# Moving the activation and the output step of an expert tile in the orders of two engines

## The chip, the cores and the metric

The kernel runs on one core of a Trainium2 chip. The metric is the device time of one execution in microseconds (us): the median of three runs before the change is 366.8 us (365.99 to 367.01). The engines that matter are TensorE (PE in the profile; PEld are its weight loads), VectorE (DVE), ScalarE (ACT), GpSimd (POOL), which starts the gathers and scatters, and SyncE (SP), which starts the other transfers. Each engine works through its own list of instructions in order, so an instruction that waits holds up all that stand behind it.

## What is computed

The input is x, 2048 tokens of 512 numbers. After a layer norm, two branches are added to x: an RWKV mixing layer (a recurrence over time for each channel) and a layer of eight experts, of which each token uses up to two, with four further "zero experts" that pass the token through.

```
xn = layernorm(x)
r, v, k = split(xn @ W_rvk.T)
y   = sigmoid(r) * wkv(time_decay, time_first, k, v)      # a recurrence over the 256 steps of each of 8 sequences
att = y @ W_out.T

probs = softmax(xn @ classifier_w.T)                      # 12 columns: 8 experts, 4 zero experts
idx   = top_k(probs + bias, 2);  w = probs[idx] * 1.5
g, u  = xn @ gate_w[e].T, xn @ up_w[e].T                  # 256 numbers for each expert e
out_e = (silu(g) * u) @ down_w[e].T
ffn   = sum over e of w[e] * out_e + xn * (sum of w over the zero experts)

return x + att + ffn
```

(In the code the reference's setup gives one sequence of 2048 tokens to the recurrence, which the kernel runs through in four blocks of 512.)

## The kernel before the change

**The start**, to about 61 us, normalises x, writes it to a scratch array xs, computes the routing, and sorts the token and expert pairs into tiles of 128 places, each tile belonging to one expert (two of them, "mixed", to two experts). The kernel works through TILES = 23 of them, and through a loop for more that is entered only if there are more.

**The long middle**, 61 to about 328 us, interleaves three streams of work.

- *Projections* (line 555, run from `pair`): k, v and r of the recurrence by a seven-product scheme. A step is one small matrix product into a PSUM bank (p1, p2, p3, pr) and a copy out of it on ScalarE (lines 574 to 599), with additions on VectorE (587, 600).
- *Scans* (`scan`, 16 units: four blocks by four groups of 128 channels): on VectorE a first part (lines 322 to 329), two exponentials on ScalarE (331, 332), then in one piece a run of VectorE work (338, 339, 340, 347 to 351) with an exponential of r on ScalarE (344) in the middle, then two reciprocals (354) and the product that gives yT (357). In the profile a scan's tiles are named obv, a, sums and yT.
- *Expert tiles*. For tile i: a gather of its rows on POOL (`gather`, 965); a copy xp on ScalarE (`flip`, 1032) and a transposing transfer on SP (1034); a copy xgT on ScalarE (`unite`, 1040); the gate and up products pg on TensorE (`up`, 1059, or 1011 for a mixed tile), 256 columns each, in one PSUM bank; the activation (`activate`): a tanh on ScalarE (1071) and two products on VectorE (1072, 1073) that read the bank and write act; the down products po (`finish`, 1007); a scaling copy yo on ScalarE (1091) and a scatter that adds it to the output (1095, POOL). Weights of the tile come by SP (986 for gate and up, 993 for down).

PSUM after the start: the bank of pg, from a pool "gu", exists once, so pg of tile i + 1 cannot begin before line 1073 of tile i has read it. The po tiles share a pool "ps_o" of two banks with the output rows pw.

**Output rows** (`attention`, line 1192 and 1180, tiles pw): y times W_out for 128 tokens, evicted on VectorE (1204) with the zero experts' share and added to the output by POOL (1165), or, for the last block, added to rows read back (1159, 1201, 1188) and written by SP.

**The order** of each engine in the middle is written out by hand (`manual_schedule`): the instructions of all engines stand in the order in which Python emits them. That order comes from a table: `plan(at, what, ...)` enters a piece of work with a planned time, and the table is sorted by it. `first_half(i)` (the fetch of weights, pg, the activation, a gather) is planned at 4 + spread * i, `second_half(i)` (unite of tile i + 1, flip of tile i + 2, finish of tile i - 1, the fetch of down weights) at 4 + spread * (i + 0.6). After the table a scheduler orders the rest, and may place some of it among the last pieces of the table.

Of the kernel before, what the change touches and what calls it, by code (L numbers as in the profile page):

```python
# [53 lines left out]
TILES = 23  # L54
# [9 lines left out]
def layer(ctx: ExitStack, tc: tile.TileContext, x, w_rvk, w_out, decay, first, cls, ebias, gu, down, out):  # L64
# [852 lines left out]
    to_i = const.tile([P, MAX_TILES], I32, tag="to_i", name="to_i")  # L917
    nc.vector.scalar_tensor_tensor(to_i, token, -float(P), empty, ALU.add, ALU.add)
    wplace = const.tile([P, MAX_TILES], F32, tag="wplace", name="wplace")
# [28 lines left out]
    st = {}  # L948
# [4 lines left out]
    def column(i):  # L953
        return seq[i] if i < TILES else 0

    def is_mixed(i):
        return i < TILES and seq[i] < MIXED
# [4 lines left out]
    def gather(i, token=token_i):  # L962

        xg = gathered.tile([P, C], F32, tag="xg", name=f"xg{i}")
        nc.gpsimd.indirect_dma_start(  # L965
            out=xg,
            out_offset=None,
            in_=xs,
            in_offset=bass.IndirectOffsetOnAxis(ap=token[:, column(i) : column(i) + 1], axis=0),
        )  # L970
        st.setdefault(i, {"w": [], "e": [], "d": []})["xg"] = xg

    def fetch(i, h=0, which=None):

        if which is None:
            k = column(i)
            which = owner_i[0:1, k, h : h + 1] if is_mixed(i) else which_i[0:1, k : k + 1]
        e = nc.values_load(
            which,
            engines=(SP,),  # L980
            min_val=0,
            max_val=E - 1,
            skip_runtime_bounds_check_because="a sum of E - 1 comparisons, or a number of one expert",
        )
        w = ewp.tile([P, CC, 2 * INTER], F32, tag="gw", name=f"gw{i}_{h}")
        nc.sync.dma_start(w, gu[bass.ds(e, 1)].rearrange("o p c n -> p (o c) n"))
        s = st.setdefault(i, {"w": [], "e": [], "d": []})
        s["w"].append(w)
        s["e"].append(e)

    def fetch_down(i, h=0):
        d = ewp.tile([P, IC, C], F32, tag="dw", name=f"dw{i}_{h}")
        nc.sync.dma_start(d, down[bass.ds(st[i]["e"][h], 1)].rearrange("o p c n -> p (o c) n"))
        st[i]["d"].append(d)
# [3 lines left out]
    def fetch_parts(what, i):  # L998

        while fetched[what] < min(ahead[i] + 3, len(parts)):  # L1000
            (fetch if what == "w" else fetch_down)(*parts[fetched[what]])
            fetched[what] += 1

    def product(i, out_, lhs, rhs, c, last):

        if not is_mixed(i):
            nc.tensor.matmul(out_, lhs[:, c, :], rhs[0][:, c, :], start=(c == 0), stop=(c == last))  # L1007
            return
        for g in range(P // GROUP):
            gs = slice(g * GROUP, (g + 1) * GROUP)  # L1010
            nc.tensor.matmul(  # L1011
                out_[gs],
                lhs[:, c, gs],
                rhs[g == P // GROUP - 1][:, c, :],
                start=(c == 0),
                stop=(c == last),
                tile_position=(0, g * GROUP),
            )

    def turn(i):  # L1020

        pt = bank("gu", f"px{i}", (CC, P))
        for c in range(CC):
            nc.tensor.transpose(pt[:, c, :], st[i]["xg"][:, c * P : (c + 1) * P], ident)
        xgT = wk1.tile([P, CC, P], F32, tag="xgT", name=f"xgT{i}")
        nc.scalar.copy(xgT, pt)
        st[i]["xgT"] = xgT
# [18 lines left out]
    def up(i, cs):  # L1046

        if 0 in cs:
            st[i]["pg"] = bank("gu", f"pg{i}", (2, INTER))
        pg = st[i]["pg"]  # L1050
        xgT, w = st[i]["xgT"], st[i]["w"]
        for c in cs:
            if is_mixed(i):
                product(i, pg, xgT, w, c, CC - 1)
                continue

            rs = slice(c * P, (c + 1) * P)
            for k in range(CC):
                nc.tensor.matmul(  # L1059
                    pg[:, c // IC, c % IC * P : (c % IC + 1) * P],  # L1060
                    w[0][:, k, rs],
                    xgT[:, k, :],
                    start=(k == 0),
                    stop=(k == CC - 1),
                )

    def activate(i):
        pg = st[i]["pg"]

        act = ex_p.tile([P, INTER], F32, tag="act", name=f"act{i}")  # L1070
        nc.scalar.activation(act, pg[:, 0, :], AF.Tanh, scale=0.5)  # L1071
        nc.vector.scalar_tensor_tensor(act, act, 1.0, pg[:, 0, :], ALU.add, ALU.mult)  # L1072
        nc.vector.tensor_mul(act, act, pg[:, 1, :])
        st[i]["act"] = act
        if not is_mixed(i):
            st[i]["actT"] = act.rearrange("p (c t) -> p c t", c=IC)

    def turn_act(i):
        pt = ps_o.tile([P, IC, P], F32, tag="o", name=f"pa{i}")
        for c in range(IC):  # L1080
            nc.tensor.transpose(pt[:, c, :], st[i]["act"][:, c * P : (c + 1) * P], ident)
        actT = wk1.tile([P, IC, P], F32, tag="actT", name=f"actT{i}")
        nc.scalar.copy(actT, pt)
        st[i]["actT"] = actT

    def finish(i, weight=wplace, to=to_i):
        po = ps_o.tile([P, C], F32, tag="o", name=f"po{i}")
        for c in range(IC):
            product(i, po, st[i]["actT"], st[i]["d"], c, IC - 1)
        yo = rows.tile([P, C], F32, tag="rb", name=f"yo{i}")  # L1090
        nc.scalar.activation(yo, po, AF.Identity, scale=weight[:, column(i) : column(i) + 1])
        k = column(i)

        def scatter(ps, index):
            nc.gpsimd.indirect_dma_start(  # L1095
                out=out,
                out_offset=bass.IndirectOffsetOnAxis(ap=index, axis=0),
                in_=yo[ps],
                in_offset=None,
                compute_op=ALU.add,  # L1100
            )


        if is_mixed(i):
            scatter(slice(0, P - GROUP), to[: P - GROUP, k : k + 1])
            held.append(lambda: scatter(slice(0, P), late_i[:, k : k + 1]))
        else:
            scatter(slice(0, P), to[:, k : k + 1])
        del st[i]
# [3 lines left out]
    def scatter_held():  # L1113
        while held:
            held.pop()()

    def first_half(i, n):

        fetch_parts("w", i)
        up(i, (0, 1))  # L1120
        if i > 0 and is_mixed(i - 1):
            turn_act(i - 1)
        up(i, (2, 3))
        activate(i)
        if i + 4 < n:
            gather(i + 4)
        scatter_held()

    def second_half(i, n):

        if i + 1 < n:
            unite(i + 1)
        if i + 2 < n:
            flip(i + 2)
        if i > 0:
            finish(i - 1)
        fetch_parts("d", i)
# [113 lines left out]
    def plan(at, what, *args):  # L1251
        table.append((at, iter([(what, *args)]) if args else what))
# [23 lines left out]
    spread = (total - 12) / TILES  # L1276
    for i in range(TILES):
        plan(4 + spread * i, first_half, i, TILES)
        plan(4 + spread * (i + 0.6), second_half, i, TILES)
    plan(6 + spread * (TILES - 1), read_xn, NTB - 2)  # L1280
    plan(7 + spread * TILES, read_xn, NTB - 1)
    plan(3 + spread * TILES, finish, TILES - 1)
    for _, work in sorted(table, key=lambda entry: entry[0]):
        todo = next(work, None)
        if todo:
            todo[0](*todo[1:])
# [10 lines left out]
    with tc.If(count > TILES):  # L1297
        with tc.For_i(TILES, MAX_TILES, 1) as i:
            cols = {}
            for name, a, dt in (  # L1300
                ("which", which_i, I32), ("token", token_i, I32), ("to", to_i, I32), ("weight", wplace, F32)
            ):
                cols[name] = small.tile([P, 1], dt, tag=f"col_{name}", name=f"col_{name}")
                nc.vector.tensor_copy(cols[name], a[:, bass.ds(i, 1)])
            gather(TILES, cols["token"])
            fetch(TILES, 0, cols["which"][0:1, 0:1])
            fetch_down(TILES)
            turn(TILES)
            up(TILES, range(CC))
            activate(TILES)  # L1310
            finish(TILES, cols["weight"], cols["to"])


    read_out(NTB - 1)
# [44 lines left out]
```

## Time and profile before

| | us |
|---|---|
| median of three runs | 366.8 (365.99 to 367.01) |
| the profiled execution | 366.11 |
| its span | 364.3 |
| TensorE busy | 354.8 (97%) |
| VectorE busy | 306.0 (84%) |
| ScalarE busy | 157.9 (43%) |
| tanh of a tile (1071), 23 times | 0.384 each |
| products of a tile (1072, 1073), 46 times | 0.415 and 0.420 each |
| scaling copy yo (1091), 23 times | 0.688 each |
| a scan's run on VectorE, 338 to 351, around 91.7 to 97.2 us | 5.5 |

How to read it: the span is the time from the first to the last recorded instruction of one execution; what lies around it is 1.8 us here. Busy time is the union of an engine's instructions. TensorE's matrix products are pipelined: an instruction in float32 is two passes, and the time that matters is the distance between the starts of passes (0.11 us for 128 columns, 0.22 for 256, 0.43 for 512), not the length of one. In a timeline a line holds the start, the length, the engine, the source line, the operation, and in brackets the idle time in front of it with what ended it; neighbouring instructions of one kind are one line ("x4"), and its length reaches to the end of the last.

### The profile page before, as it was taken

What the parts mean: (1) busy time and instruction counts of PE and PEld (TensorE: products, weight loads), DVE (VectorE), ACT (ScalarE), POOL (GpSimd) and SP (SyncE); (2) the same over time, 40 slices, a digit from 0 to 9 for tenths busy, and PEclk for the clock granted to TensorE, in tenths of its full rate; (3) what the DMA queues carried; (4) which work ended last, traced back from release to release, by engine and by line L of the source; (5) the groups of instructions that cost most, each with busy time, mean ns of one, the idle gap of its engine ahead of it and who ended that gap; (6) DMA issues with size and microseconds to landing.
All of it is one profiled execution on the core that took longest, in us unless ns stands there. A gap on an engine that the chain in (4) does not pass through costs nothing.

```text
span 364.3 us, 5277 instructions
## 1 busy us (share of the span) xinstructions
PE 354.8 (97%) x1840; PEld 253.9 (70%) x1840; DVE 306.0 (84%) x524; ACT 157.9 (43%) x303; POOL 89.5 (25%) x118
## 2 busy tenths in 40 slices
PE   8999999999989999999999999999999999999996
PEld 3565468798856877558866788887777888864444
DVE  5889989988999597898699959799968599879971
ACT  1667122345455345553535454546543446432000
POOL 6000200421302332332321242333223332122130
PEclk9999999999999999999999999999999999999999
DMA  8999941895848999799999599878989978934782
GB/s 270 395 376 352 347 146 21 321 288 126 222 151 258 271 291 269 182 281 259 314 285 235 164 259 254 247 134 289 245 285 252 266 160 187 349 56 57 172 129 106
DMA packets 47133, 84.46 MB, mean 232 GB/s; under 512 B 26497, under 2 KB 26881, under 8 KB 43329
## 3 DMA queue, kind: packets, MB, share of 16 engines
q1 hardware_dynamic: 39792, 64.05, 54.7%
q0 software_dynamic: 7312, 20.06, 25.6%
q8 instruction: 15, 0.25, 0.3%
q14 instruction: 14, 0.11, 0.1%
HBM read 63.25 MB, written 19.27 MB: 227 GB/s over the span
## 4 chain that ended last, share of the span: by engine, by line
PE 51%; DVE 25%; ACT 3%; DMA 2%; issue 2%; POOL 1%; SPq 0%; DVEq 0%; ACTq 0%
PE pg L1059 16%; PE p L555 12%; PE pw L1192 8%; PE po L1007 6%; DVE sums L354 5%; PE pr L555 5%; DMA gw<-in_gu_dram 2%; DVE sums L340 2%; DVE sums L338 2%; DVE obv L326 2%; DVE sums L349 1%; DVE yT L357 1%; DVE sums L350 1%; DVE a L351 1%; PE po L1011 1%
## 5 line engine op out<-in xcount | busy, mean ns | idle before, releaser
L1059 PEld LDWEIGHTS pg<-xgT,gw 128*128 128x128 f32 x672 | 78.2, 192 | 4.1 <-issue 1.9
L1059 PE MATMUL pg<-xgT,gw 128*128 128x128 f32 x672 | 79.0, 275 | 0.4 <-DMA gw<-in_gu_dram 0.4
L1095 POOL DMA_INDIRECT out_dram<-yo,to_i x23 | 39.4, 1713 | 145.2 <-DMA out_dram<-yo,to_i 31.0
L1192 PE MATMUL pw<-wout_sb,yT 128*128 128x512 f32 x120 | 54.5, 595 | 0.8 <-DVE xrows L1204 0.4
L354 DVE RECIPROCAL sums<-sums 128x256 f32<-128x256 f32 x32 | 54.7, 1731 | 0.0
L1192 PEld LDWEIGHTS pw<-wout_sb,yT 128*128 128x128 f32 x120 | 22.2, 190 | 26.9 <-issue 25.4
L1007 PE MATMUL po<-dw,act 128*128 128x512 f32 x84 | 39.5, 592 | 0.0
L965 POOL DMA_INDIRECT xg<-xs,token_i x23 | 26.2, 1138 | 45.8 <-DVE empty L916 25.2
L1071 ACT ACTIVATE act<-pg 128x256 f32<-128x256 f32 x23 | 8.8, 384 | 65.7 <-PE pg L1059 60.5
L1072 DVE SCALAR_TENSOR_TENSOR act<-act,pg 128x256 f32<-128x256 f32 x23 | 9.5, 415 | 26.3 <-ACT act L1071 26.3
L338 DVE TENSOR_TENSOR_SCAN sums<-obv,state,a 128x512 f32<-128x512 f32 x16 | 20.5, 1281 | 7.1 <-ACT obv L332 7.0
L1040 ACT COPY xgT<-xq 128x1024 uint16<-128x1024 uint16 x22 | 25.6, 1162 | 0.0
L555 PE MATMUL p<-S,T 128*128 128x256 f32 x96 | 24.9, 382 | 0.3 <-ACT v L578 0.3
L1007 PEld LDWEIGHTS po<-dw,act 128*128 128x128 f32 x84 | 16.0, 190 | 13.3 <-issue 12.2
L555 PE MATMUL p<-S,wrvk 128*128 128x256 f32 x96 | 24.7, 380 | 0.4 <-DVE S L408 0.4
L555 PE MATMUL p<-xnT,wrvk 128*128 128x256 f32 x96 | 24.7, 379 | 0.0
L1032 ACT COPY xp<-xg 128x1024 uint16<-128x1024 uint16 x22 | 23.0, 1047 | 1.0 <-DMA xg<-xs,token_i 1.0
L555 PEld LDWEIGHTS p<-S,T 128*128 128x128 f32 x96 | 17.9, 190 | 6.8 <-issue 2.4
L340 DVE TENSOR_TENSOR_SCAN sums<-obv,state,a 128x512 f32<-128x512 f32 x16 | 20.5, 1284 | 0.6
L555 PEld LDWEIGHTS p<-S,wrvk 128*128 128x128 f32 x96 | 17.7, 190 | 4.2 <-issue 1.2
L326 DVE TENSOR_TENSOR_SCAN obv<-wdec,state,k 128x512 f32<-128x512 f32 x16 | 20.5, 1279 | 0.0
L555 PEld LDWEIGHTS p<-xnT,wrvk 128*128 128x128 f32 x96 | 17.8, 190 | 3.4 <-issue 1.2
(262 smaller groups left out, 571.8 us busy)
## 6 DMA issues: line engine op xcount, KB each, us to landing
gw<-in_gu_dram SPq DMA_DIRECT2D x25, 1024.0 KB, 7.9
dw<-in_down_dram SPq DMA_DIRECT2D x25, 512.0 KB, 4.3
x<-in_x_dram SPq DMA_DIRECT2D x16, 256.0 KB, 5.3
xs<-x SPq DMA_DIRECT2D x16, 256.0 KB, 4.2
wrvk<-in_w_rvk_dram SPq DMA_DIRECT2D x3, 1024.0 KB, 8.5
xrow<-xs SPq DMA_DIRECT2D x8, 256.0 KB, 5.9
out_dram<-xrow POOLq DMA_DIRECT2D x8, 256.0 KB, 8.1
xrows<-xs SPq DMA_DIRECT2D x8, 256.0 KB, 6.2
```

What stands on the lines that cost most here:

```text
L326: nc.vector.tensor_tensor_scan(o2, w.to_broadcast([P, TB]), k, s[:, 0:1], ALU.add, ALU.max)
L338: nc.vector.tensor_tensor_scan(sq, bs, a2, s[:, 3:4], ALU.add, ALU.mult)
L340: nc.vector.tensor_tensor_scan(sp, bvs, a2, s[:, 4:5], ALU.add, ALU.mult)
L354: nc.vector.reciprocal(den[:, hs], den[:, hs])
L555: nc.tensor.matmul(dst, rows_(k), a[:, k, :], start=(first and k == 0), stop=(k == 1), skip_group_check=True,)
L965: nc.gpsimd.indirect_dma_start(out=xg, out_offset=None, in_=xs, in_offset=bass.IndirectOffsetOnAxis(ap=token[:, column(i) : column(i) + 1] ...
L1007: nc.tensor.matmul(out_, lhs[:, c, :], rhs[0][:, c, :], start=(c == 0), stop=(c == last))
L1032: nc.scalar.copy(xp, st[i]["xg"].bitcast(U16).rearrange("p (c h) -> p h c", h=2))
L1040: nc.scalar.copy(xgT.bitcast(U16).rearrange("p c (t h) -> p c t h", h=2), st[i]["xq"].rearrange("p (h c) t -> p c t h", h=2),)
L1059: nc.tensor.matmul(pg[:, c // IC, c % IC * P : (c % IC + 1) * P], w[0][:, k, rs], xgT[:, k, :], start=(k == 0), stop=(k == CC - 1),)
L1095: nc.gpsimd.indirect_dma_start(out=out, out_offset=bass.IndirectOffsetOnAxis(ap=index, axis=0), in_=yo[ps], in_offset=None, compute_op=ALU ...
L1192: nc.tensor.matmul(po, yT[b][:, c, j * P : (j + 1) * P], wout_sb[:, c, :], start=(c == 0), stop=(c == CC - 1),)
```

## The change

The activation leaves `first_half` and gets an entry of its own in the table, 3.6 planned us after the start of the half, and the scaling copy and the scatter leave `finish` as a new function `send`, planned 1.9 after the half that holds the down products. TensorE's work keeps its order but for the end.

```diff
-    def finish(i, weight=wplace, to=to_i):
+    def finish(i):
         po = ps_o.tile([P, C], F32, tag="o", name=f"po{i}")
         for c in range(IC):
             product(i, po, st[i]["actT"], st[i]["d"], c, IC - 1)
+        st[i]["po"] = po
+
+    def send(i, weight=wplace, to=to_i):
+        po = st[i]["po"]
         yo = rows.tile([P, C], F32, tag="rb", name=f"yo{i}")
         nc.scalar.activation(yo, po, AF.Identity, scale=weight[:, column(i) : column(i) + 1])
...
         up(i, (2, 3))
-        activate(i)
         if i + 4 < n:
             gather(i + 4)
...
     for i in range(TILES):
         plan(4 + spread * i, first_half, i, TILES)
+
+        plan(4 + spread * i + 3.6, activate, i)
         plan(4 + spread * (i + 0.6), second_half, i, TILES)
+        if i > 0:
+            plan(4 + spread * (i + 0.6) + 1.9, send, i - 1)
...
     plan(3 + spread * TILES, finish, TILES - 1)
+    plan(5 + spread * TILES, send, TILES - 1)
...
-            finish(TILES, cols["weight"], cols["to"])
+            finish(TILES)
+            send(TILES, cols["weight"], cols["to"])
```

What it does to the orders, read from the two built programs:

- VectorE: the two products of a tile stand behind up to ten instructions that stood behind them (9 at tile 1, 6 at tiles 6, 9, 10 and 19, 10 at tile 14, 7 at tile 22, none at tiles 7, 11, 17 and 20). At tiles 1, 9, 14, 19 and 22, for example, these include a scan's run from 338 to 351.
- ScalarE: the tanh stands behind up to five instructions more, yo behind up to three.
- POOL: one scatter, that of tile 6, stands behind the additions of two output rows (1165) that stood behind it. The rest is as before.
- SP: as before.
- TensorE: as before, but that the first two products of the very last row half (pw_last, line 1180) stand in front of po of the last tile instead of at the end, and two products of pw of row tile 11 stand behind the branch to the loop of further tiles instead of in front of it.

## The prediction

> **What bounds the kernel now.** I read the busy shares first, then the sums by stretch, the waits, and the timeline around the few places where TensorE stood still. The profiled execution took 366.11 us, 364.3 of it the span; the runs' median is 366.8.
>
> ```profile
> PE 354.8 (97%) x1840; PEld 253.9 (70%) x1840; DVE 306.0 (84%) x524; ACT 157.9 (43%) x303; POOL 89.5 (25%) x118
> ```
>
> ```profile
> 186.00:252.00 66.00, 65.67 (x363) 53.33 (x362) 57.87 (x83) 31.56 (x61) 19.88 (x15) 1.00 0.87 232
> 252.00:322.00 70.00, 70.00 (x393) 57.13 (x394) 57.82 (x81) 33.89 (x64) 18.63 (x14) 1.00 0.88 238
> ```
>
> The second view gives, after the length of a stretch, the busy time of PE, of its weight loads, DVE, ACT and POOL. From 186 to 322 us PE is full: 135.67 of 136.00. A later VectorE or ScalarE costs nothing until PE waits for it, and an earlier one can give back only what PE now waits.
>
> ```profile
> ACT act L1071 <- PE pg L1059: 60.5, 20, 5.4
> ...
> DVE act L1072 <- ACT act L1071: 26.3, 13, 3.8
> ```
>
> These are the waits that the change goes for: ScalarE stands 60.5 us in front of the tanh, VectorE 26.3 us in front of the first product after it. Neither is PE's time.
>
> **What it takes away.** What PE loses I read from the starts of its groups: four passes of line 555 follow each other 0.86 us after their start, four of line 1192 after 1.72 (both in the chain of waits). After 75 us there are six places of note. (a) At 90.84 us line 555 starts 0.50 late, for the copy of v (L578), and the moved tanh holds 0.27 of ScalarE in front of that copy (90.16 to 90.43): 0.25 falls away. (b) pg of tile 3 starts at 107.97, and 105.72 + 0.86 is 106.58: 1.39, for xgT (L1040), which stands behind the two exponentials of a scan and so behind its L328 and the products of tile 2 (102.35). With that pair (two of 0.42 us, 0.8) out of the way, and the run in front of it earlier by 0.5 (1.4 gained at its start, 0.9 taken back for tile 1's pair, below), xgT ends 1.3 earlier, at 106.6, while PE now comes 0.6 later (below), at 107.2: all of 1.39 goes. (c) pg of tile 4, 119.96 against 118.55 + 0.86: 0.55, for weights whose transfer follows xp (L1032) and its transpose through SP's queue; those move with xgT, 1.3 earlier, PE only 0.8: it goes. (d) pw at 195.86 against 194.57 + 0.86: 0.43, for xrow (L1204), behind tile 10's products (191.62). (e) pg of tile 16, 251.97 against 250.88 + 0.86: 0.23, like (b). (f) pw at 346.84 against 344.51 + 1.72: 0.61, for the row evictions L1204 behind the last scan; there PE now comes later than VectorE. Together 0.25 + 1.39 + 0.55 + 0.43 + 0.23 + 0.61 = 3.46 us. That is the whole purse.
>
> **What it adds.** No instruction is new; 23 tanhs of 0.38 us, 46 products of 0.42 and 23 copies yo of 0.69 move. Two things wait for the products: the next tile's pg, since the pool "gu" holds one bank and L1073 is its last reader, and the tile's own po (L1007). In the order of VectorE the pair now often stands behind a scan's whole run, L338 to L351, which was queued behind it.
>
> ```profile
> 90.84 1.13 PE L555 MATMUL p<-S,T 128*128 128x256 f32 x4 [0.33 <-ACT v L578]
> ...
> 91.69 1.27 DVE L338 TENSOR_TENSOR_SCAN sums<-obv,state,a 128x512 f32<-128x512 f32 x1
> ...
> 96.12 3.73 PE L1059 MATMUL pg<-xgT,gw 128*128 128x128 f32 x32
> ...
> 96.50 0.74 DVE L351 SCALAR_TENSOR_TENSOR a<-obv,cfac,sums 128x512 f32<-128x512 f32 x1
> ```
>
> (g) Tile 2. The run can start when L332 ends (89.63 + 0.63 = 90.26), 1.4 earlier than 91.69; so L351 ends at 97.24 - 1.4 = 95.84, and with the pair (0.88 from the first's start to the second's end, 90.56 to 91.44) the bank is free at 96.7. PE comes at 96.12 - 0.25 = 95.87. New wait: 0.9. It makes PE 0.6 late at tile 3, which (b) and (c) turn into 1.3 early.
>
> ```profile
> 181.46 1.28 DVE L338 TENSOR_TENSOR_SCAN sums<-obv,state,a 128x512 f32<-128x512 f32 x1 [1.03 <-ACT obv L332]
> ...
> 186.36 0.75 DVE L351 SCALAR_TENSOR_TENSOR a<-obv,cfac,sums 128x512 f32<-128x512 f32 x1
> ...
> 186.69 3.73 PE L1059 MATMUL pg<-xgT,gw 128*128 128x128 f32 x32
> ```
>
> (h) Tile 10. Here the run cannot start earlier against PE: its exponentials stand behind a ScalarE copy (L599, 180.01) that waits for PE. L351 ends 0.42 after PE comes for pg (187.11 against 186.69); with the pair (0.8 behind it) that is 1.2. What (b) and (c) gave is gone. (i) Tile 15 is a tie: VectorE's run ends 1.1 after PE comes (L351, 242.37 against 241.28) but starts some 2 earlier (it loses a 2.35 us wait for the tanh at 234.13), and two short operations follow: 0 to 0.5, I take 0.1.
>
> ```profile
> 322.08 0.37 ACT L595 COPY r<-pr 128x256 f32<-128x256 f32 x1 [0.48 <-PE pr L555]
> ...
> 323.54 1.28 DVE L338 TENSOR_TENSOR_SCAN sums<-obv,state,a 128x512 f32<-128x512 f32 x1 [0.70 <-ACT obv L332]
> ...
> 326.17 1.88 PE L1007 MATMUL po<-dw,act 128*128 128x512 f32 x4
> ...
> 328.09 0.75 DVE L351 SCALAR_TENSOR_TENSOR a<-obv,cfac,sums 128x512 f32<-128x512 f32 x1
> ```
>
> (j) The last tile is the largest. Its products ran at 321.63 to 322.51, while VectorE waited for the exponentials anyway; in the new order they follow L351. That run is tied to PE by the copy at 322.08. L351 ends at 328.84, the pair at 329.65; po of tile 22, at 326.17 until now, has the first two steps of the very last row tile put in front of it (four passes of 256 columns, 0.86) and so is reached at 327.03. New wait: 2.6. The two steps are work taken from the end, neither gain nor loss. What follows, 19 steps of line 1192 of 0.86 each, has no other slack than (f).
>
> New waits: 0.9 + 1.2 + 0.1 + 2.6 = 4.8. The sum: 4.8 - 3.46 = 1.3 us, 364.3 to 365.6 for the span, 366.8 to 368.1 for the median.
>
> **Costed at nothing.** The later yo and its scatter: the bank of po is one of two and is wanted again a tile (11 us) later, and scatters wait on POOL anyway (yo of 174.23 is scattered at 187.99, after 8.56 us for an earlier transfer). Tile 6's scatter now stands behind two row additions (L1165), before it in front. POOL's next gather moves with this: ScalarE waited once, 0.96 us at 239.57, for a gather. Without the cover I bound this part by that wait from above, and by its loss from below: -1 to +1.
>
> [...] The starts decide: line 1059 starts a pass every 0.11 us (32 in 3.57) though a load takes 0.19, so loads overlap and their share is no measure of room. [...]
>
> **The rivals.** One, on the other side: the run on VectorE comes earlier than I allow, and (g), (h), (i) don't arise. For it: 26.3 us of waits leave VectorE. Against: at tile 10 and at the end the run is released by ScalarE copies that wait for PE, not for VectorE. 366.8 - 3.46 + 2.6 = 365.9, and 363.3 if the end's wait too were covered; it decides if L351 of that run ends 1.2 us earlier against PE. Two, a draw: one wait of the size of (h) fails to come, 366.9. Three, worse: VectorE's lateness spreads. Reckoned as above, the pair is within about 1 us of PE at tiles 6, 7 and 11; one half to one microsecond at two of them adds 1.5: 369.6. That the change doesn't do what it says is no rival of weight: in the orders of the built program 21 of 23 tanhs, 19 pairs and 17 copies yo stand behind work that was behind them, up to ten instructions for a pair.
>
> **The numbers.** Forecast 368.1, chance 0.42 (own range 367.6 to 368.8); the draw 0.30; worse 0.14; faster side 0.14. One measurement tells about 0.3%, 1.1 us: slower starts at 367.9, faster ends at 365.7. Slower: 0.36 of the forecast's and all of the worse, 0.50; faster: 0.12 of the faster side; same: 0.38. The range, with the -1 to +1 of POOL's part: 366.0 to 369.7.
>
> **What would show it.** Each in the profile after: ScalarE's 60.5 and VectorE's 26.3 us in front of the moved lines mostly gone, with no gain in span; PE waiting for DVE act (L1073) at pg near 96 and 186 us and at po near 327, the last by 2.6; no wait near 107, 119 and 347. I am wrong if PE's last wait is under 1.5 us, if waits at pg come at more than four tiles, or if a gather or weight transfer becomes what PE waits for.

## The result, and the profile after

The changed kernel takes 369.77 us, the median of 19 executions (367.71 to 372.87); the kernel before took 365.99 in 19 executions beside it (364.88 to 368.49). The ratio is 1.0105, with a 95% interval of 1.0082 to 1.0127: slower by 1%, or 3.8 us. The forecast was 368.1 with a range up to 369.7, so the direction was right, the size was not, and the result lies just beyond the range. The forecast counted from 366.8; from there the range reached 2.9 us up, and 3.8 was measured against the kernel beside it, so the miss of the change is larger than that of the time.

The profiled execution took 372.09 us, 370.3 of it the span, 6.0 us more than the 364.3 before. First the page: busy time of each engine, and in 40 equal slices of the span the clock that TensorE was granted, in tenths.

```profile
PE 358.1 (97%) x1840; PEld 255.7 (69%) x1840; DVE 306.4 (83%) x524; ACT 156.8 (42%) x303; POOL 87.3 (24%) x118
...
PEclk9899999999999999999999999999999999998999
```

The number of passes is the same (1840), yet PE's busy time has grown from 354.8 to 358.1. Work that doesn't change and takes longer points at the clock, and the last line has two slices with an 8, the second of all and the fourth from the end; the profile before has none.

Next the waits (in total, times, longest), for what the change aimed at.

```profile
ACT k L595 <- PE p L555: 25.2, 10, 8.4
...
DVE sums L338 <- ACT obv L332: 17.9, 8, 6.7
...
DVE act L1072 <- ACT act L1071: 16.1, 6, 4.6
...
ACT act L1071 <- PE pg L1059: 4.1, 3, 2.8
```

ScalarE's 60.5 us in front of the tanh are down to 4.1, VectorE's 26.3 in front of the first product to 16.1. The waits went elsewhere: ScalarE now stands 25.2 us in front of its copy of k (8.1 before), and VectorE 17.9 in front of a scan (7.0 before). Neither sets the end. PE does, and in its timeline (start, length, engine, line, operation, in brackets the idle time in front and what ended it) the new waits stand where they were looked for:

```profile
98.87 1.35 PE L1059 MATMUL pg<-xgT,gw 128*128 128x128 f32 x10 [0.89 <-DVE act L1073]
...
108.55 1.03 PE L555 MATMUL p<-xnT,wrvk 128*128 128x256 f32 x4
109.50 3.64 PE L1011 MATMUL pg<-gw,xgT 128*32 128x512 f32 x32
...
189.06 3.81 PE L1059 MATMUL pg<-xgT,gw 128*128 128x128 f32 x32 [1.30 <-DVE act L1073]
...
243.69 2.58 PE L1059 MATMUL pg<-xgT,gw 128*128 128x128 f32 x21 [0.33 <-ACT yo L1095]
...
328.33 1.03 PE L1183 MATMUL pw_last<-wout_sb,yT 128*128 128x256 f32 x4
331.88 3.48 PE L1007 MATMUL po<-dw,act 128*128 128x512 f32 x4 [2.52 <-issue]
335.16 14.97 PE L1195 MATMUL pw<-wout_sb,yT 128*128 128x512 f32 x34
```

By the starts of the passes these are 1.06, 1.47, 0.50 and 2.68 us late: 5.71. At 109.50 pg of tile 3 no longer waits for xgT: 0.95 after the start of the four passes in front of it, against 2.25 before (105.72 to 107.97). The line of before:

```profile
107.97 1.50 PE L1011 MATMUL pg<-gw,xgT 128*32 128x512 f32 x12 [1.22 <-ACT xgT L1040]
```

The bracket at 331.88 names "issue", that at 243.69 a copy; VectorE's own timeline shows the true releaser of both. At the last tile the pair stands behind L351, at the end of the scan's run, and its second product ends at 331.78, 0.10 before po starts. At 243.69 it ends 0.26 before pg starts, as it does at 98.87 and 189.06.

```profile
243.01 0.42 DVE L1073 TENSOR_TENSOR act<-act,pg 128x256 f32<-128x256 f32 x1
...
327.60 1.28 DVE L340 TENSOR_TENSOR_SCAN sums<-obv,state,a 128x512 f32<-128x512 f32 x1
...
330.25 0.75 DVE L351 SCALAR_TENSOR_TENSOR a<-obv,cfac,sums 128x512 f32<-128x512 f32 x1
330.91 0.41 DVE L1072 SCALAR_TENSOR_TENSOR act<-act,pg 128x256 f32<-128x256 f32 x1
331.36 0.42 DVE L1073 TENSOR_TENSOR act<-act,pg 128x256 f32<-128x256 f32 x1
```

Now the length at 331.88: four passes of po take 3.48 us, and the same four took 1.88 before. The sums by stretch tell why. They are cut where the record of the clock changes, at steps of 3.41 us; the columns are the stretch, its length, busy time (and instructions) of PE, its weight loads, DVE, ACT and POOL, the granted clock, the DMA share and GB/s.

```profile
325.34:328.75 3.41, 3.41 (x10) 1.70 (x9) 3.02 (x3) 1.80 (x4) 2.06 (x1) 1.00 0.00 0
328.75:332.16 3.41, 0.89 (x4) 0.49 (x3) 3.26 (x7) 0.00 (x0) 0.00 (x0) 1.00 0.59 77
332.16:335.57 3.41, 3.41 (x5) 1.35 (x4) 3.38 (x3) 0.17 (x1) 1.54 (x1) 0.50 0.37 40
335.57:338.98 3.41, 3.41 (x9) 1.50 (x8) 3.37 (x6) 1.60 (x3) 0.93 (x1) 1.00 0.21 37
```

PE stands 2.52 us in the second stretch, and for the whole third stretch its clock is one half: five passes, where the busy stretches, the first and the fourth, hold ten and nine. The starts of those passes are 0.85 us apart instead of 0.43; together the starts lose 1.77 us. The wait is paid once as idle time and again as a slow restart.

The other 8 belongs to 11.31 to 14.72 us, the same 3.41 us at half clock, in the first transposes. The change doesn't touch them; by 70 us PE is 1.83 us behind the kernel before. So 5.8 of the 6.0 us between these two profiles are accounted for: 1.83 at the start, 5.71 of new waits, 1.77 of slow passes behind the last one, less the 3.5 that were taken away.

Each execution lists its span and mean clock. One stretch of 3.41 us at one half in 366 is a mean of 0.995, two make 0.991, so the executions can be sorted by the number of falls. Median span, and executions in brackets:

| kernel | clock 0.997 and over | 0.993 to 0.996 | 0.991 and under |
|---|---|---|---|
| before (beside the experiments) | 364.0 (39) | 366.4 (13) | none |
| after | 366.4 (7) | 368.4 (9) | 370.3 (3) |

At full clock the change costs 2.4 us; the remaining 1.4 of the 3.8 is that 12 of its 19 executions have one or two falls, and only 13 of 52 of the kernel before.

### The profile page after: what moved, and what is told of

Its sections match the earlier page's. It is cut to its first block, busy times and chain, and to the rows that moved or that the text cites. A ratio compares the mean times of both kernels' runs of the same rounds, so it can differ in the third digit from the quotient of the medians.

```text
span 370.3 us, 5289 instructions
## 1 busy us (share of the span) xinstructions
PE 358.1 (97%) x1840; PEld 255.7 (69%) x1840; DVE 306.4 (83%) x524; ACT 156.8 (42%) x303; POOL 87.3 (24%) x118
## 5 line engine op out<-in xcount | busy, mean ns | idle before, releaser
L1007 PE MATMUL po<-dw,act 128*128 128x512 f32 x84 | 41.1, 613 | 2.5 <-issue 2.5
L338 DVE TENSOR_TENSOR_SCAN sums<-obv,state,a 128x512 f32<-128x512 f32 x16 | 20.6, 1285 | 18.1 <-ACT obv L332 17.9
L965 POOL DMA_INDIRECT xg<-xs,token_i x23 | 24.4, 1060 | 46.9 <-DVE empty L916 25.2
L1072 DVE SCALAR_TENSOR_TENSOR act<-act,pg 128x256 f32<-128x256 f32 x23 | 9.5, 414 | 16.3 <-ACT act L1071 16.1
L555 PEld LDWEIGHTS p<-S,T 128*128 128x128 f32 x96 | 17.9, 190 | 6.4 <-issue 2.2
L1095 ACT ACTIVATE yo<-po,wplace 128x512 f32<-128x512 f32 x23 | 15.9, 692 | 10.2 <-PE po L1007 10.2
```

The costliest lines, as they stand in the source:

```text
L338: nc.vector.tensor_tensor_scan(sq, bs, a2, s[:, 3:4], ALU.add, ALU.mult)
L555: nc.tensor.matmul(dst, rows_(k), a[:, k, :], start=(first and k == 0), stop=(k == 1), skip_group_check=True,)
L965: nc.gpsimd.indirect_dma_start(out=xg, out_offset=None, in_=xs, in_offset=bass.IndirectOffsetOnAxis(ap=token[:, column(i) : column(i) + 1] ...
```

## The experiments

Eight kernels, in two groups of four, each group on one chip beside the kernel before. The theory, called W: what is lost lies at the last tile, in PE's wait for products that stand behind a scan's run on VectorE, and in the clock that falls behind this wait. Rivals: the clock falls by chance whatever PE does (C); the loss is spread over the tiles (S).

**The last tile alone in its old place.**

```diff
         up(i, (2, 3))
+        if i == TILES - 1:
+            activate(i)
...
-        plan(4 + spread * i + 3.6, activate, i)
+        if not (i == TILES - 1):
+            plan(4 + spread * i + 3.6, activate, i)
```

> The changed kernel, but the last tile's tanh and products stand where they stood before, directly after its pg; all else as changed. Theory W (wait and clock): what the changed kernel lost by its end is the wait of po of tile 22 (2.68 us by the starts of PE's passes) and, in the executions whose granted clock falls to half behind that wait, another 1.77 us (the four passes that start 0.85 instead of 0.43 apart). Both go; the wait of 0.61 us at line 1192, which the later PE had covered, comes back. From the changed kernel's executions at clock 1.0 (span about 366.2): 366.2 - 2.68 + 0.61 = 364.1, time about 365.9, ratio to the kernel before 0.998 to 1.001, and no fall of the clock in the last 40 us. Rival C (the clock falls by chance, whatever PE does): the fall behind 330 us stays in half or more of the executions, time 366.5 to 367.5. Rival S (the loss is spread over the tiles): the time stays within 1 us of the changed kernel, 368.8 or more.

Measured: 366.43 us (12 executions), ratio 1.0018 (0.9999 to 1.0037); 11 of 12 at full clock, the profiled span 364.4. PE reaches po of tile 22 without a wait; the two steps of the very last row tile that the change puts in front of it stand at the end again, which by itself is neither gain nor loss.

```profile
326.28 1.88 PE L1007 MATMUL po<-dw,act 128*128 128x512 f32 x4
```

The loss is gone, so it was the last tile's. The time is half a microsecond above what W gave; the other 22 tiles together are no gain: the waits at pg of tiles 2, 10 and 15 (1.06, 1.46 and 0.30 by the starts, 2.8 together) eat the 2.8 taken away elsewhere, and the row wait of 0.52 near 346 us is back as expected. S falls.

**The last tile alone late, the rest as before.**

```diff
         up(i, (2, 3))
-        activate(i)
+        if i < TILES - 1:
+            activate(i)
...
+        if i == TILES - 1:
+            plan(4 + spread * i + 3.6, activate, i)
```

> The kernel before, but the last tile alone has its tanh and products later; yo, the scatters and all other tiles as before. Theory W: po of tile 22 waits 2.6 to 3.4 us for the products, 0.61 of it comes back at line 1192; where the clock falls behind the wait, 1.8 more. Span 364.3 + 2.0 to 2.8 = 366.3 to 367.1 at full clock, 368.1 to 368.9 with the fall, time 368 to 370.5, ratio 1.006 to 1.012. Rival C: 1.005 to 1.008 and no more falls of the clock than the kernel before shows beside it. Rival S: no difference of note, below 1.003.

Measured: 368.73 us (6 executions), ratio 1.0080 (1.0058 to 1.0102), within W's bounds, and at the upper end of C's: one late tile of 23 gives 2.8 us. The profile has the same wait and no fall behind it.

```profile
330.14 1.96 PE L1007 MATMUL po<-dw,act 128*128 128x512 f32 x4 [2.52 <-issue]
```

Here the steps of the clock's record cut the wait in two:

```profile
326.20:329.61 3.41, 1.42 (x6) 0.72 (x4) 3.27 (x5) 0.00 (x0) 2.29 (x1) 1.00 0.20 18
329.61:333.03 3.42, 2.89 (x7) 1.44 (x8) 3.41 (x3) 0.69 (x1) 0.00 (x0) 1.00 0.37 59
```

PE works 1.42 us in the first of the two stretches, against 0.89 where the clock fell. So the wait costs its 2.68 us in both, and the clock falls behind it in one of the two profiles alone. They differ in where the idle time lies against the steps: from 329.36 to 331.88 us within one step there, from 327.62 to 330.14 across the edge at 329.61 here. Two of six executions show a clock of 0.994, which by itself doesn't tell W from C.

**The wait filled with work.**

```diff
         po = ps_o.tile([P, C], F32, tag="o", name=f"po{i}")
+        if i == TILES - 1:
+            for c in (0, 1, 2):
+                nc.tensor.matmul(po, st[i]["xgT"][:, c, :], st[i]["d"][0][:, 0, :], start=True, stop=True)
```

> The changed kernel with three matmuls of 128x512 added in front of po of tile 22 (six passes of 0.43 us, 2.58 us), from xgT and the first part of dw into the same bank, which the first real pass overwrites; the result is the same. PE's wait of 2.5 us is filled with work, so that the products are as late as before but PE never stands. Theory W: the clock does not fall behind 330 us, and every execution costs what the changed kernel's did at full clock: span 366.0 to 366.7, time about 368.0, ratio 1.004 to 1.007. Rival C (the fall has nothing to do with the wait): as the changed kernel, a median near 369.8, ratio 1.009 to 1.012, with falls as often. If the added passes are themselves in the way (they start later than reckoned), the time is above 369.8 at full clock.

Measured: 369.53 us (6 executions), ratio 1.0097 (1.0073 to 1.0121). The time is W's miss and lies in C's range, but not for C's reason: the added passes took the place of four passes of 256 columns of the very last row tile, which went back to the end (0.86 us), and still left a wait of 0.76, so at full clock it is 367.6 instead of 366.4. But the clock did what W says: in the profile it doesn't fall behind 330 us (its one fall lies in the second of the 40 slices, between 9.2 and 18.5 us, at the start), and five of six executions are at 0.999 or 1.0, where 7 of 19 of the changed kernel were. The lines are the granted clock in 40 slices, the added passes and po:

```profile
PEclk9899999999999999999999999999999999999999
...
328.13 2.74 PE L1090 MATMUL po<-dw,xgT 128*128 128x512 f32 x6
331.63 1.99 PE L1007 MATMUL po<-dw,act 128*128 128x512 f32 x4 [0.76 <-DVE act L1073]
```

Filling a wait with useless work kept the clock and won nothing here.

**A longer wait.**

```diff
         nc.vector.tensor_mul(act, act, pg[:, 1, :])
+        if i == TILES - 1:
+            for _ in range(4):
+                nc.vector.tensor_copy(act, act)
```

> The changed kernel with four more VectorE copies of act of tile 22 onto itself behind its products (0.42 us each by the rows of the products, 1.7 in all); the result is the same. PE's wait in front of po of tile 22 grows from 2.7 to 4.4 us. Theory W (a long enough wait lets the clock fall): the granted clock falls behind the wait in nearly every execution, where it fell in somewhat over half of the changed kernel's; span 366.2 + 1.7 + 1.8 = 369.7, time 371.3 to 372.0, mean clock 0.995 or below in five of six. Rival C (the clock falls by chance): 0.995 in a fifth of the executions, as in the kernel before beside it, span 367.9, time 369.4 to 370.2.

Measured: 372.14 us (6 executions), ratio 1.0130 (1.0084 to 1.0176). Five of six executions are at 0.995 or below, three of them at 0.991. C, which had 369.4 to 370.2 and a fifth of the executions, falls. The copies took 0.3 us each, so the wait grew by 1.3:

```profile
331.45 3.75 PE L1007 MATMUL po<-dw,act 128*128 128x512 f32 x4 [3.83 <-issue]
```

and in the sums by stretch:

```profile
326.57:329.98 3.41, 1.05 (x5) 0.57 (x3) 3.27 (x6) 0.00 (x0) 1.92 (x1) 1.00 0.31 32
329.98:333.39 3.41, 1.94 (x3) 0.94 (x4) 3.27 (x7) 0.00 (x0) 0.00 (x0) 0.50 0.26 45
333.39:336.80 3.41, 3.41 (x6) 1.34 (x5) 3.34 (x5) 0.69 (x1) 0.60 (x1) 0.50 0.00 0
```

The half clock lasts two steps here: the wait reaches into a second one, in which PE is busy for only 1.94 us at the slow rate, and the step behind it is at one half as well.

**The tanh and its products moved, yo and its scatter not; and the reverse.**

```diff
         st[i]["po"] = po
+        if i < TILES:
+            send(i)
...
-        if i > 0:
-            plan(4 + spread * (i + 0.6) + 1.9, send, i - 1)
...
-    plan(5 + spread * TILES, send, TILES - 1)
```

> The changed kernel, but yo and the scatter stand directly behind the down products again: only the tanh and its products are moved. Theory W with the prediction's zero for the rest: no difference from the changed kernel, span 366.2 at full clock and 1.8 more with a fall, time 368.0 to 369.8, ratio to the kernel before 1.005 to 1.011. Rival P (yo, the scatter and what they move on POOL's queue have a price of their own, at most 1 us either way): at full clock 1 us less, 367.0, or 1 us more, 369.0.

```diff
         up(i, (2, 3))
+        activate(i)
...
-        plan(4 + spread * i + 3.6, activate, i)
```

> The kernel before with yo and the scatter planned later, as in the changed kernel; the tanh and its products stay. Theory W: no difference, ratio 0.998 to 1.002, the same waits of PE at pg of tiles 3, 4 and 16. Rival P: 1.003 or more, or 0.997 or less, with a gather or a copy as what PE newly waits for.

Measured: the tanh alone 370.25 us (10 executions), ratio 1.0103 (1.0065 to 1.0141); yo and the scatter alone 366.50 (10 executions), ratio 1.0003 (0.9968 to 1.0037). All of the loss is the tanh's and the products'; the first kernel's time is 0.4 above W's range, its ratio inside. Its spans at full clock, at one fall and at two are 366.4, 368.3 and 370.2 (2, 4 and 4 executions), the changed kernel's own 366.4, 368.4 and 370.3. The profile of the tanh alone repeats the sequence of a wait and a fall:

```profile
327.10:330.51 3.41, 0.89 (x4) 0.44 (x3) 3.27 (x6) 0.00 (x0) 1.79 (x1) 1.00 0.04 7
330.51:333.92 3.41, 3.41 (x6) 1.36 (x5) 3.38 (x5) 0.69 (x1) 0.00 (x0) 0.50 0.55 77
```

**Other work in front of the last tile's down products.**

```diff
-    plan(3 + spread * TILES, finish, TILES - 1)
-    plan(5 + spread * TILES, send, TILES - 1)
+    plan(7 + spread * TILES, finish, TILES - 1)
+    plan(9 + spread * TILES, send, TILES - 1)
```

> The changed kernel, but the last tile's down products are planned four steps later and its yo and scatter with them, so that passes of line 1195 stand in front of po of tile 22 and PE has its own work while VectorE makes the products. Theory W: the wait of 2.7 us shrinks to below 1, the clock does not fall behind it, span 364.0 to 365.0, time 365.8 to 366.8, ratio 0.999 to 1.003. Rival E (the end is set by the last tile's scatter and the rows read behind it, which come later now): ratio 1.005 or more with PE waiting at the last rows instead. Rival C: falls of the clock behind 330 us as often as in the changed kernel.

Measured: 366.91 us (12 executions), ratio 1.0015 (0.9987 to 1.0043); 10 of 12 at full clock. The products are as late as in the changed kernel, but PE does four passes of line 1195 first; 1.24 us of the wait are left, more than expected, and in the profile there is no fall behind it. The time is 0.1 above W's range, the ratio inside.

```profile
331.87 1.96 PE L1007 MATMUL po<-dw,act 128*128 128x512 f32 x4 [1.24 <-issue]
```

Neither the later yo nor the later scatter lengthened the end.

**Four tiles in their old places.** The condition of the first experiment, with more tiles:

```diff
+        if i in (1, 9, 14, TILES - 1):
+            activate(i)
...
-        plan(4 + spread * i + 3.6, activate, i)
+        if not (i in (1, 9, 14, TILES - 1)):
+            plan(4 + spread * i + 3.6, activate, i)
```

> The changed kernel, but tiles 1, 9, 14 and 22 have their tanh and products where they stood before: those whose later products PE waited for (pg of tiles 2, 10 and 15, po of 22). Theory W with the prediction's sum: the waits near 98, 188, 243 and 330 us go (1.06 + 1.47 + 0.50 + 2.68 by the starts), the waits removed at pg of tiles 3 and 4 (1.39 + 0.55) stay removed, the others (a, d, e, f of the prediction) come back with the old order: 364.3 - 1.94 = 362.4 for the span, time 363.9 to 364.6, ratio 0.994 to 0.997. Rival: what is won at tiles 3 and 4 is lost again before the end to the next wait (a transfer or a copy), ratio 0.998 to 1.001. Rival S: 1.003 or more.

Measured: 364.33 us (12 executions; the ratio leaves out one of 369.51 us), ratio 0.9951 (0.9925 to 0.9976): 0.5% faster than the kernel before, with a median span of 362.2 at full clock against 364.0. Where PE paid, it no longer does: pg of tile 10 follows its predecessor without a wait.

```profile
105.16 1.03 PE L555 MATMUL p<-xnT,wrvk 128*128 128x256 f32 x4
106.63 3.64 PE L1011 MATMUL pg<-gw,xgT 128*32 128x512 f32 x32 [0.44 <-ACT xgT L1040]
...
118.71 1.46 PE L1059 MATMUL pg<-xgT,gw 128*128 128x128 f32 x11 [0.48 <-DMA gw<-in_gu_dram]
...
182.87 2.74 PE L1197 MATMUL pw<-wout_sb,yT 128*128 128x512 f32 x6
185.44 2.73 PE L1059 MATMUL pg<-xgT,gw 128*128 128x128 f32 x23
```

Two of the removed waits are back, that at tile 3 by half and that at tile 4 in full: by the starts pg of tile 3 is 0.61 late for xgT (1.39 before), and pg of tile 4 is 0.65 late for its weights (0.55 before). That tile 1's pair, in front again, is the reason fits the prediction's sum for (b) and wasn't tried by itself. In return the waits (d) and (e), which were expected back, stay away. The profiled span is 2.1 below the 364.3 before, for an expected 1.94, but the closeness is luck: 0.6 of the 2.1 lies ahead of 70 us, which the change doesn't touch, and the waits behind give 1.5 by the starts.

## Why the prediction was wrong in size

**What the profile was read for held.** TensorE is the bound; ScalarE's and VectorE's waits in front of the moved lines went without a gain; what decides is where PE newly waits. The last wait was forecast as 2.6 and is 2.68, of VectorE's products behind L351, at the place named. What fell away is the 3.5 us read from PE's starts; the busy share of the weight loads, 70% of the span before and 69% after, was no measure of it.

**What it takes away.** (b), (c), (d), (e) and (f) are gone in the profile after, by the starts 1.39, 0.55, 0.43, 0.22 and 0.54; of (a) 0.37 went. Together 3.5, against 3.46.

**What it adds: each size a little low, by a term put at nothing.** (g) 0.9 is 1.06; (h) 1.2 is 1.47; (i) 0.1 is 0.50 in the profile after, about 0.3 in those of the experiments. The sum is 5.7 (5.5 with the smaller one) for 4.8. The net, forecast as 1.3, is 2.2 by the waits and 2.4 by the spans at full clock. The prediction let PE start when the pair ends. In the profile after, the first pass of pg starts 0.26 us after the second product's end at tiles 2, 10 and 15, and po of tile 22 starts 0.10 after it; together 0.88 of the 0.91 that the waits were forecast too low. Up to the end of the pair (g), (h) and (j) come out within 0.1 of the forecast. For (i) it is 0.24 in the profile after; one more operation, L587, stood in front of the pair. No pass in the profile before waited for L1073, so it had no row for the 0.26. (Counted in the profiles, the pair of tile 9 stands behind eight instructions more and that of tile 14 behind twelve, not six and ten: the two short copies of a scan's state, lines 347 and 348, belong to the run. The sums went by the run's length and don't change.)

**The step that failed: what follows the last wait.** "What follows, 19 steps of line 1192 of 0.86 each, has no other slack than (f)": the passes behind the wait were counted at the full rate. In the profile after, five of them run at half the rate, 1.77 us more, and this happens in most executions: if the falls at the start come as often as in the kernel before (13 in 52), then about 20 of 29 executions of the two kernels with this tail (27 falls in all) fall behind the wait, an estimate. The profile of before has one record of half clock, which begins 1.9 us after the last work, and the longest time for which PE stands between two passes in it is 1.22 us (in front of pg of tile 3), so it held no case of a wait of 2.5 us; but the prediction didn't ask what a wait does to the clock, and none of its signs of being wrong was about it. With the clock at one (7 executions, span 366.4), the kernel is 0.8 us above the forecast's span of 365.6; the 368.2 that this makes in time is inside the forecast's own range, helped by the base of 366.8, which was 0.8 above the 365.99 measured beside the change. So of the 3.8 us, 1.3 were forecast, about 1 is the low sizes, and 1.4 is the clock.

**Costed at nothing.** Rightly, within the intervals: yo and the scatter moved alone give 1.0003 (0.9968 to 1.0037), and left in place they make no difference that shows (1.0103 against 1.0105).

**The rivals.** The faster side and the draw are excluded by the interval. "Worse", lateness that spreads to tiles 6, 7 and 11, named 369.6, close to the measured time for a reason that isn't there: no wait arises at those tiles.

## What to carry to other kernels

An operation moved later in an in-order engine lands behind whatever is long in that engine's order; it costs where the bound engine needs its result, and there it should be kept early: four of 23 tiles in their old places turned a loss of 1.0% into a gain of 0.5%. Price a new wait of the bound engine twice, once as idle time and once for the slower passes behind it: here 2.5 us of idle time cost up to 1.8 more. Add what passes between the end of the producer and the first pass of the consumer, 0.26 us here. If the producer can't be made earlier, put real work of the bound engine in front of the wait; the filling passes tried here kept the clock, but took the time that they filled.

## What the runs showed of the hardware

In the profile after, the half-clock records are 3.41 us long, but for the last, which the end of the trace cuts off, and they lie on one grid (11.31 and 332.16 us are 94.0 steps apart); with the longer wait the half clock lasted two such steps, 329.98 to 336.80 us. The grid lies differently in each of these profiles: near the last tile a step begins at 328.75 us in the profile after, at 329.61 with the last tile alone late, at 329.98 with the longer wait and at 327.10 with the tanh alone moved. There, a step in which PE was busy for 0.89 or 1.05 us was followed by one at half clock (three profiles), one with 1.42 us was not (one profile).

Busy time alone doesn't draw the line: in the first transposes, the step with 1.86 us of the profile after (7.90 to 11.31 us) was followed by half clock, though that with 1.42 us near the last tile was not; one with 1.97 us in the kernel before (7.79 to 11.20) was not either. The lengths of passes overlap (a transpose of 128 columns is 0.27 us long and the next starts 0.11 after it, 512 columns in float32 0.59 and 0.43), so busy time counts them too high. Counted by the distances between starts (0.11, 0.22 and 0.43 us in float32, 0.22 for the 512 columns of the bfloat16 passes at the start), the three steps near the last tile that one at half clock follows hold about 0.7 to 0.9 us of passes, and the one at the start of the profile after 1.23. The step with 1.42 us of busy time holds 1.25, that at the start of the kernel before 1.33, and the one of its last products (359.36 to 362.77 us) 1.31; none of these was followed by half clock. So, as an estimate from these counts, PE keeps its clock here if a step of 3.41 us holds passes for somewhat over a third of its length (1.25 us were enough, 1.23 were not), and a wait costs the clock by where it lies on the grid as well as by its length.

A quarter of the executions of the kernel before (13 of 52) carry a clock of 0.994 or 0.995 and are 2.4 us longer. Two profiles show the half clock in the first transposes: the profile after, from 11.31 us, and that with other work in front of the last down products, where the mean clock is 0.53 from 11 to 14.5 us; that of the filled wait has it in the second of its 40 slices. In the first two PE stands 1.28 and 1.84 us in front of the first transposes; in the kernel before and with the tanh alone moved, where the clock is 1.00 there, it stands 1.17 and 0.31. That the slower executions of the kernel before fell there too fits, and isn't shown: none of them was profiled.
